# Two further expert-weight buffers laid over dead tiles in a one-core decoder layer with a routed feed-forward

## The chip, the cores and the metric

The kernel runs on one core of a Trainium2 chip. The core has a matrix engine (PE, with PEld for its weight loads), a vector engine (DVE), a scalar engine (ACT), GpSimd (POOL) and a queue engine (SP) that here only issues DMAs. The metric is the device time of one execution in microseconds (us); smaller is better. Engines run on their own and wait for each other through semaphores; each works through its own list of instructions in a fixed order.

## What is computed

A pre-norm decoder layer on 1024 tokens of width 512, all in float32. Cut to its three steps:

```python
x = x + attn(layernorm(x))                 # self-mixing over the batch axis
x = x + cross_attn(layernorm(x), ctx)      # 32 query heads, 8 key heads
x = x + ffn(layernorm(x))

def ffn(x):                                # x: 1024 x 512
    scores = sigmoid(x @ gate_w.T) + bias  # 16 experts
    w, idx = top_k(scores, 4); w = w / (w.sum() + 1e-20)
    out = sum over the 4 chosen experts e of  w_e * (silu(x @ Wg[e].T) * (x @ Wu[e].T)) @ Wd[e].T
    return out + silu(x @ Sg.T) * (x @ Su.T) @ Sd.T      # the shared expert
```

The change is about the routed experts. Each expert has three matrices of 512 KB (`Wg`, `Wu`, `Wd`), 1.5 MB together.

## The kernel before, in words

The program is written in a tile language: the author writes the operations in a source order, and a scheduler decides at build time in which order each engine's instructions stand and which semaphores they wait for. The order of the built program therefore need not be the order of the source, and a change in one engine's work can move instructions on another.

**Up to about 769 us** the two attention steps and the routing run. `xnT` (L101) is a 128 x 4 x 1024 tile that holds the normed tokens turned round; its last reader is the shared expert's first product (L885). `acc` (L102) is a 128 x 8 x 512 tile that holds the token sums; its last readers are the DMAs that write the layer's base result to the output (L904). Both tiles belong to the pool `keep` and stay allocated to the end.

**Routing** gives each expert the list of its tokens, cut into blocks of 128. There are at least 32 (`SURE`) and at most 47 (`NB`) blocks. On the first partition the kernel computes, per block, the expert's number and a flag `fresh` (L942 to L952): 1 where the weights must be loaded, 0 where the buffer already holds that expert. Both go into `steer`, which SP reads before each load.

**The main blocks** are the 32 sure ones (loop L1057 to L1070). They are taken in four lanes: step `j` works on block `8 * (j % 4) + j // 4`, with weight buffer `j % 4`. Neighbouring blocks of a lane mostly belong to one expert, so most loads have `fresh` 0 and are skipped. Step `j` has these parts on PE:

- X(j+1): four transposes of the gathered token rows `xg` into PSUM (L1005); ACT copies them to `xt` (L1007).
- Z(j-1): two transposes of the hidden rows `z` (L1025); DVE copies them to `zt` (L1027).
- H(j): the product of `xt` with `w1` (`Wg` and `Wu`), L1014; ACT takes the silu (L1018), DVE multiplies (L1019), which gives `z`.
- C(j-1): the product of `zt` with `w2` (`Wd`), L1034; ACT scales it to `y` (L1038).

POOL then touches `y` (L1041) and scatters it with an accumulating indirect DMA into the output (L1042); each scatter waits until the one before has landed. POOL also gathers the rows of later blocks (L996). X and Z share two PSUM banks (`tr`), which they take in turn, so the next X cannot start before ACT has copied the last X out of its bank.

**Loads.** `load_expert(j)` reads the expert's number and flag on SP and issues three conditional DMAs (L986) into `w1` and `w2` of the buffer; SP waits there until PE has finished with what the buffer held. At step `j` the load for step `j + 3` is issued. There are four buffers (`WB`, L970 and L971).

**The further blocks** (32 to 46) may or may not exist; they are done two at a time inside nested conditionals (`further`, L1083). They use the same four buffers, `(j - 1) % 4`. The load of block 33 stands at step 30 of the main loop, those of blocks 32, 34 and 35 behind the loop (L1067 to L1072), and inside `further` the loads of the two blocks after the next two stand behind the work of the pair (L1093). Block 32 shares its buffer with the last main block, so its flag compares its expert with that block's.

```python
def block(j):
    return SURE // WB * (j % WB) + j // WB if j < SURE else j
def buffer(j):
    return j % WB if j < SURE else (j - 1) % WB
```

Of the kernel before, what the change touches and what calls it, by code (L numbers as in the profile page):

```python
# [26 lines left out]
ALU = mybir.AluOpType  # L27
AX = mybir.AxisListType

P = 128  # L30
N, C, L = 16, 64, 512
NT = N * C // P
DC = L // P
KVH, GRP, HD = 8, 4, 128
E, FI = 16, 256
# [6 lines left out]
NB = 47  # L42
SURE = 32
WB = 4
ROUND = float(3 << 22)
HIGHEST = 3.0e38

# [2 lines left out]
def decoder_layer(  # L50
# [25 lines left out]
    V, S, T, G = nc.vector, nc.scalar, nc.tensor, nc.gpsimd  # L76
# [24 lines left out]
    xnT = keep.tile([P, DC, NT * P], F32, tag="xnT", name="xnT")  # L101
    acc = keep.tile([P, NT, L], F32, tag="acc", name="acc")  # L102
# [333 lines left out]
    for u in range(NT // 2):  # L436
        s = work.tile([P, 3, 2, P], F32, tag=f"xns{u}", name="xns", bufs=1)
# [310 lines left out]
    def routed_pair(u):  # L748
# [64 lines left out]
        V.tensor_scalar(col, got, 1.0 / P, (P - 1) / (2.0 * P), ALU.mult, ALU.subtract)  # L813
        V.tensor_scalar(col, col, ROUND, ROUND, ALU.add, ALU.subtract)
        row = route.tile([P, 2 * TOPK], F32, tag="row", name="row", bufs=1)
# [90 lines left out]
    def shared_half(th, queue):  # L906
# [33 lines left out]
    expert = route.tile([1, NB + 1], F32, tag="expert", name="expert")  # L940
    V.tensor_copy(expert, bp[:1, 128 : 128 + NB + 1])
    fresh = route.tile([1, NB + 1], F32, tag="fresh", name="fresh")  # L942
    V.memset(fresh, 1.0)
    runs, turns = (t[:, :SURE].rearrange("o (w r) -> o w r", w=WB) for t in (expert, fresh))
    V.tensor_tensor(turns[:, :, 1:], runs[:, :, 1:], runs[:, :, : SURE // WB - 1], ALU.not_equal)
    V.tensor_tensor(
        fresh[:, SURE : SURE + 1], expert[:, SURE : SURE + 1], expert[:, SURE - 1 : SURE], ALU.not_equal
    )
    V.tensor_tensor(
        fresh[:, SURE + WB :], expert[:, SURE + WB :], expert[:, SURE : NB + 1 - WB], ALU.not_equal  # L950
    )
    V.tensor_mul(fresh, fresh, bp[:1, 192 : 192 + NB + 1])  # L952
    in_use = route.tile([1, 1], F32, tag="inuse", name="in_use")
# [15 lines left out]
    moe = ctx.enter_context(tc.tile_pool(name="moe", bufs=2))  # L969
    w1_tiles = [moe.tile([P, 2, DC, FI], F32, tag=f"w1{b}", name="w1", bufs=1) for b in range(WB)]  # L970
    w2_tiles = [moe.tile([P, FI // P, L], F32, tag=f"w2{b}", name="w2", bufs=1) for b in range(WB)]  # L971

    def block(j):
        return SURE // WB * (j % WB) + j // WB if j < SURE else j

    def buffer(j):
        return j % WB if j < SURE else (j - 1) % WB

    def load_expert(j):
        b = block(j)  # L980
        e = nc.sync.value_load(steer[0:1, 0, b : b + 1], min_val=0, max_val=E - 1)
        new = nc.sync.value_load(steer[0:1, 1, b : b + 1], min_val=0, max_val=1)
        for dst, src in (
            (w1_tiles[buffer(j)][:, 0], wg), (w1_tiles[buffer(j)][:, 1], wu), (w2_tiles[buffer(j)], wd),
        ):
            nc.sync.dma_start(  # L986
                dst, src[bass.ds(e, 1)].rearrange("o p c f -> p (o c) f"), cond=(new != 0)
            )
# [4 lines left out]
    def gathered(j):  # L993
        b = block(j)
        xg = moe.tile([P, L], F32, tag="xg", name="xg", bufs=6) if j < SURE else xg_further[j % 4]
        G.indirect_dma_start(  # L996
            xg, None, rows_d, bass.IndirectOffsetOnAxis(idx[:, b : b + 1], axis=0)
        )
        return xg

    def rows_turned(j):
        xg = xgs.pop(j)
        tp = tr_bank()
        for d in range(DC):
            T.transpose(tp[:, d * P : (d + 1) * P], xg[:, d * P : (d + 1) * P], ident)  # L1005
        xt = moe.tile([P, DC, P], F32, tag="xt", name="xt", bufs=3) if j < SURE else xt_further[j % 4]
        S.copy(xt.rearrange("p d t -> p (d t)"), tp)  # L1007
        xts[j] = xt

    def hidden(j):  # L1010
        xt = xts.pop(j)
        hp = sc_bank()
        for d in range(DC):
            T.matmul(  # L1014
                hp, xt[:, d, :], w1_tiles[buffer(j)][:, :, d, :], start=(d == 0), stop=(d == DC - 1)
            )
        z = moe.tile([P, FI], F32, tag="z", name="z", bufs=3)
        S.activation(z, hp[:, :FI], AF.Silu)  # L1018
        V.tensor_mul(z, hp[:, FI:], z)  # L1019
        return z  # L1020

    def hidden_turned(z):
        tp = tr_bank()
        for c in range(FI // P):
            T.transpose(tp[:, c * P : (c + 1) * P], z[:, c * P : (c + 1) * P], ident)  # L1025
        zt = moe.tile([P, FI // P, P], F32, tag="zt", name="zt", bufs=3)
        V.tensor_copy(zt.rearrange("p c t -> p (c t)"), tp[:, :FI])  # L1027
        return zt

    def combined(j, zt):  # L1030
        b = block(j)
        op = mm_bank()
        for c in range(FI // P):
            T.matmul(  # L1034
                op, zt[:, c, :], w2_tiles[buffer(j)][:, c, :], start=(c == 0), stop=(c == FI // P - 1)
            )
        y = moe.tile([P, L], F32, tag="y", name="y", bufs=6)
        S.activation(y, op, AF.Copy, scale=weight[:, b : b + 1])  # L1038

        mark = xg_further[j % 4][:, :1] if SURE - 8 <= j < SURE - 4 else seen  # L1040
        G.tensor_copy(mark, y[:, :1])  # L1041
        G.indirect_dma_start(  # L1042
            out, bass.IndirectOffsetOnAxis(idx[:, b : b + 1], axis=0), y, None,
            bounds_check=NT * P - 1, oob_is_err=False, compute_op=ALU.add,
        )
# [11 lines left out]
    for j in range(SURE + 1):  # L1057
        if j + AHEAD < LAST:
            xgs[j + AHEAD] = gathered(j + AHEAD)
        rows_turned(j + 1)  # L1060
        zt = hidden_turned(zs.pop(j - 1)) if j > 0 else None
        if j < SURE:
            zs[j] = hidden(j)
        if zt is not None:
            combined(j - 1, zt)

        if j + WB - 1 < SURE:  # L1067
            load_expert(j + WB - 1)
        elif j == SURE - WB + 2:
            load_expert(SURE + 1)  # L1070
    for j in (SURE, SURE + 2, SURE + 3):
        load_expert(j)  # L1072

    blocks_used = nc.values_load(
        count[0:1, 0:1],
# [7 lines left out]
    def further(j0):  # L1083
        pair, later, last = ([j for j in (j0 + k, j0 + k + 1) if j < NB] for k in (0, 2, 4))
        with tc.If(blocks_used > j0):  # L1085
            for j in last:
                xgs[j] = gathered(j)
            for j in pair:
                z = hidden(j)
                if j + 2 < NB:  # L1090
                    rows_turned(j + 2)
                combined(j, hidden_turned(z))
            for j in last:  # L1093
                load_expert(j)
            if later:
                further(j0 + 2)

    further(SURE)


# [50 lines left out]
```

## Time and profile before

| what | value |
|---|---|
| time, median of 6 runs | 1000.67 us (998.75 to 1001.95) |
| the profiled execution's own time | 999.99 us |
| its span, first to last instruction | 998.2 us |
| mean granted PE clock | 0.995 |
| PE busy | 948.7 us (95% of the span) |
| DVE, ACT, POOL busy | 550.0, 441.7, 334.4 us |
| main blocks, PE (first H to the end of the loop) | 770.3 to 960.2 us |
| further blocks, PE | 960.2 to 985.1 us |
| scatters, gathers, load triples | 36, 40, 40 |

With 36 scatters, 36 blocks are in use: the 32 sure ones and four further ones (32 to 35). Of the 40 load triples most are skipped: on SP a DMA that is carried out takes about 0.34 us to issue, a skipped one about 0.08 us.

How to read it: a row of the timeline gives the start, the duration, the engine, the line, the operation, output <- input, and in brackets how long the engine had been idle before and what ended that. In a table of windows each engine has its busy time and number of instructions in that stretch, then come the PE clock (1.00 is full), the DMA engines' busy share and the rate. In a table of groups the idle time before a group's instructions stands last, with what ended it. Matmuls are pipelined, so the start of the next one, not the end of the last, tells how long one took.

### The profile page before, as it was taken

The numbers are of one execution on the slowest core, as the hardware profiler recorded it, in microseconds if no ns is written. First come the engines' busy times: TensorE is split into PE (matmuls) and PEld (weight loads), VectorE is DVE, ScalarE is ACT, GpSimd is POOL, SyncE is SP. The second block draws the span as 40 slices with busy tenths as digits, with TensorE's granted clock in tenths as the row PEclk, the third lists the DMA queues.
The fourth block names the chain that finished last, engine by engine and source line by source line (L and its number), as shares of the span: only waits on it lengthen the run. The fifth ranks groups of instructions, "written<-read, shape, count | busy, mean of one in ns | idle before, by whom it ended". The sixth has DMA issues, their size and how long they took to land. (4 is left out here: it accounts for less than half of the span.)

```text
span 998.2 us, 14858 instructions
## 1 busy us (share of the span) xinstructions
PE 948.7 (95%) x5080; PEld 659.1 (66%) x5080; DVE 550.0 (55%) x1194; ACT 441.7 (44%) x1258; POOL 334.4 (34%) x356
## 2 busy tenths in 40 slices
PE   8999998999999999999999989988999899999994
PEld 3456555888888888888888877776754445445442
DVE  4565657876767676758667667678574111111110
ACT  2366672654444454544544565655530222222221
POOL 2131102341613426135243242033053444444433
PEclk9999999999999999999999999999999999999997
DMA  9120015200201102012020110000034966655763
GB/s 238 70 96 22 11 33 104 107 2 1 85 1 43 43 1 86 1 54 85 1 85 1 44 43 1 22 23 22 22 105 159 349 147 150 156 108 119 195 178 67
DMA packets 28960, 76.88 MB, mean 77 GB/s; under 512 B 4624, under 2 KB 9024, under 8 KB 26832
## 3 DMA queue, kind: packets, MB, share of 16 engines
q1 hardware_dynamic: 18160, 52.96, 15.8%
q0 software_dynamic: 10432, 22.66, 10.7%
q8 instruction: 42, 0.69, 0.3%
q10 hardware_dynamic: 288, 0.26, 0.1%
q14 instruction: 38, 0.31, 0.1%
HBM read 102.31 MB, written 14.97 MB: 117 GB/s over the span
## 5 line engine op out<-in xcount | busy, mean ns | idle before, releaser
L1014 PE MATMUL sc<-w,xt 128*128 128x512 f32 x288 | 130.2, 593 | 2.8 <-DMA w<-in_wu_dram 2.8
L467 ACT ACTIVATE square<-qraw 128x128 f32<-128x128 f32 x256 | 79.0, 308 | 65.8 <-DVE qraw L463 38.7
L1014 PEld LDWEIGHTS sc<-w,xt 128*128 128x128 f32 x288 | 51.9, 190 | 54.3 <-issue 54.3
L229 POOL TENSOR_TENSOR sat<-at 128x256 f32<-128x256 f32 x24 | 17.5, 728 | 202.6 <-ACT at L580 202.6
L1019 DVE TENSOR_TENSOR z<-sc,z 128x256 f32<-128x256 f32 x36 | 15.3, 425 | 124.4 <-ACT z L1018 118.5
L255 PE MATMUL mm<-wq_sb,xnT 128*128 128x256 f32 x256 | 72.5, 389 | 0.0
L255 PE MATMUL mm<-wo_sb,at 128*128 128x256 f32 x256 | 66.0, 382 | 5.9 <-ACT at L580 5.9
L1034 PE MATMUL mm<-w,zt 128*128 128x512 f32 x144 | 68.0, 594 | 1.6 <-DVE zt L1027 1.6
L255 PE MATMUL mm<-wq_t,xns 128*128 128x256 f32 x256 | 66.3, 381 | 2.6 <-POOL wq_t L237 1.5
L1042 POOL DMA_INDIRECT out_dram<-y,idx x36 | 57.3, 1592 | 33.7 <-DMA out_dram<-y,idx 27.6
L255 PE MATMUL mm<-wo_t,sat 128*128 128x256 f32 x256 | 67.5, 383 | 0.0
L996 POOL DMA_INDIRECT xg<-rows_d,idx x40 | 39.6, 990 | 78.7 <-PE tr L1025 55.3
L840 POOL DMA_INDIRECT table_d<-entry_sb,at_slot x24 | 26.4, 1102 | 106.3 <-DVE at_slot L807 99.9
L1018 ACT ACTIVATE z<-sc 128x256 f32<-128x256 f32 x36 | 13.8, 383 | 107.2 <-PE sc L1014 104.5
L255 PEld LDWEIGHTS mm<-wo_sb,at 128*128 128x128 f32 x256 | 48.0, 190 | 13.9 <-ACT at L580 7.7
L255 PEld LDWEIGHTS mm<-wq_t,xns 128*128 128x128 f32 x256 | 48.4, 190 | 9.7 <-POOL wq_t L237 1.9
L255 PEld LDWEIGHTS mm<-wo_t,sat 128*128 128x128 f32 x256 | 47.6, 190 | 7.0 <-DVE sat L230 0.8
L1034 PEld LDWEIGHTS mm<-w,zt 128*128 128x128 f32 x144 | 27.1, 190 | 35.3 <-issue 32.0
L580 ACT COPY at<-sc 128x512 f32<-128x512 f32 x64 | 34.3, 588 | 31.6 <-PE sc L574 31.4
L493 DVE TENSOR_TENSOR qraw<-qraw,rs 128x512 f32<-128x512 f32 x64 | 47.9, 754 | 0.4
L255 PEld LDWEIGHTS mm<-wq_sb,xnT 128*128 128x128 f32 x256 | 44.4, 190 | 5.6 <-DVE su L459 0.3
L467 ACT ACTIVATION_READ_ACCUMULATOR square<-qraw 128x1 f32 x256 | 47.7, 186 | 0.0
(289 smaller groups left out, 2070.0 us busy)
## 6 DMA issues: line engine op xcount, KB each, us to landing
w<-in_wg_dram SPq DMA_DIRECT2D x40, 512.0 KB
w<-in_wu_dram SPq DMA_DIRECT2D x40, 512.0 KB
w<-in_wd_dram SPq DMA_DIRECT2D x40, 512.0 KB
wq_sb<-in_wq_dram SPq DMA_DIRECT2D x8, 1024.0 KB
wo_sb<-in_wo_dram SPq DMA_DIRECT2D x8, 1024.0 KB
xs<-in_x_dram SPq DMA_DIRECT2D x8, 256.0 KB
wv_sb<-in_wv_dram SPq DMA_DIRECT2D x2, 1024.0 KB
ct<-in_ctxt_dram SPq DMA_DIRECT2D x8, 256.0 KB
```

The costliest lines, as they stand in the source:

```text
L229: engine.tensor_add(s[:, 0], a21, a22)
L255: T.matmul(dst, left[:, k, :], right[:, k, :], start=k == 0, stop=k == 1)
L467: S.activation(square, raw[:, h, :], AF.Square, accum_out=q_ss[g][:, 2 * u + j, h : h + 1])
L493: V.tensor_mul(raw, raw, q_rs[g, i // 2][:, i % 2, :].unsqueeze(2).to_broadcast([P, GRP, HD]))
L580: S.copy(at[:, :, b * C : (b + 1) * C], pv[b].rearrange("p (a q) -> p a q", a=2 * GRP))
L840: G.indirect_dma_start(tables_d[q], bass.IndirectOffsetOnAxis(at_slots[u][:, q : q + 1], axis=0), entry_sb[:, 2 * u + j, k, :], None,)
L996: G.indirect_dma_start(xg, None, rows_d, bass.IndirectOffsetOnAxis(idx[:, b : b + 1], axis=0))
L1014: T.matmul(hp, xt[:, d, :], w1_tiles[buffer(j)][:, :, d, :], start=(d == 0), stop=(d == DC - 1))
L1018: S.activation(z, hp[:, :FI], AF.Silu)
L1019: V.tensor_mul(z, hp[:, FI:], z)
L1034: T.matmul(op, zt[:, c, :], w2_tiles[buffer(j)][:, c, :], start=(c == 0), stop=(c == FI // P - 1))
L1042: G.indirect_dma_start(out, bass.IndirectOffsetOnAxis(idx[:, b : b + 1], axis=0), y, None, bounds_check=NT * P - 1, oob_is_err=False, comp ...
```

## The change

Two more weight buffers are added. They take no new memory: each is cut out of a tile that is no longer needed (`xnT` and `acc`; 12 KB of the 16 KB that each has per partition). The further blocks use all six buffers (`WF`), `(j - 32 + 4) % 6`: block 32 the one over `xnT`, block 33 the one over `acc`, 34 to 37 the four old ones. So the flags change: blocks 32 to 37 are always loaded if they exist, and later ones are compared with the block six before; one small DVE instruction falls away. The loads move in the source: block 32's to step 16 and block 33's to step 18 of the main loop, 34's and 35's to steps 29 and 30, and those inside `further` ahead of the pair's work.

```diff
 SURE = 32
 WB = 4
+WF = 6
...
     V.tensor_tensor(turns[:, :, 1:], runs[:, :, 1:], runs[:, :, : SURE // WB - 1], ALU.not_equal)
     V.tensor_tensor(
-        fresh[:, SURE : SURE + 1], expert[:, SURE : SURE + 1], expert[:, SURE - 1 : SURE], ALU.not_equal
-    )
-    V.tensor_tensor(
-        fresh[:, SURE + WB :], expert[:, SURE + WB :], expert[:, SURE : NB + 1 - WB], ALU.not_equal
+        fresh[:, SURE + WF :], expert[:, SURE + WF :], expert[:, SURE : NB + 1 - WF], ALU.not_equal
     )
...
+    for spare in (xnT, acc):
+        flat = spare.rearrange("p a b -> p (a b)")
+        w1_tiles.append(flat[:, : 2 * DC * FI].rearrange("p (s d f) -> p s d f", s=2, d=DC))
+        w2_tiles.append(flat[:, 2 * DC * FI : 2 * DC * FI + FI // P * L].rearrange("p (c l) -> p c l", l=L))
...
     def buffer(j):
-        return j % WB if j < SURE else (j - 1) % WB
+        return j % WB if j < SURE else (j - SURE + WB) % WF
...
         if j + WB - 1 < SURE:
             load_expert(j + WB - 1)
-        elif j == SURE - WB + 2:
-            load_expert(SURE + 1)
-    for j in (SURE, SURE + 2, SURE + 3):
-        load_expert(j)
+        elif j < SURE - 1:
+            load_expert(j + WB + 1)
+        if j in (SURE // 2, SURE // 2 + 2):
+            load_expert(SURE + (j - SURE // 2) // 2)
...
             for j in last:
                 xgs[j] = gathered(j)
+                load_expert(j)
             for j in pair:
                 z = hidden(j)
                 if j + 2 < NB:
                     rows_turned(j + 2)
                 combined(j, hidden_turned(z))
-            for j in last:
-                load_expert(j)
             if later:
                 further(j0 + 2)
```

Three lines are added ahead of L1014 in sum, so L1014 of the kernel before is L1017 of the changed one, and so on for the lines of the block loop.

## The prediction

> **What bounds the kernel now.** I read the table of windows first, to see which engine is full in the stage that the change touches. Columns after the window: its length, then PE, PEld, DVE, ACT and POOL busy, the PE clock, the DMA share, GB/s.
>
> ```profile
> 769.00:790.00 21.00, 17.88 (x61) 9.03 (x60) 3.24 (x7) 5.23 (x10) 7.57 (x10) 1.00 1.03 401
> 790.00:957.80 167.80, 167.80 (x521) 83.37 (x519) 24.21 (x57) 44.18 (x86) 77.15 (x84) 1.00 0.60 146
> 957.80:985.20 27.40, 25.78 (x77) 12.19 (x76) 3.82 (x9) 7.03 (x14) 12.83 (x14) 1.00 0.64 184
> ```
>
> From 790 to 957.8 us PE is busy 167.80 of 167.80 us: it never waits for a weight load, and whatever delays PE there delays the end. The groups of PE in the third window say what its 1.6 us of idle time are:
>
> ```profile
> L1014 PE MATMUL sc<-w,xt 128*128 128x512 f32 x32 | 14.7, 593 | 0.0
> L1034 PE MATMUL mm<-w,zt 128*128 128x512 f32 x20 | 9.7, 608 | 1.6 <-DVE zt L1027 1.6
> ```
>
> Product H, the first reader of a load, waits 0.0 us; the 1.6 us are three waits of C for DVE's copy, no load. SP's timeline shows when the further loads go out (0.08 us is a skipped DMA, 0.34 us one carried out):
>
> ```profile
> 955.50 0.08 SPq L986 DMA_DIRECT2D w<-in_wg_dram  x1
> ...
> 960.79 0.34 SPq L986 DMA_DIRECT2D w<-in_wg_dram  x1
> ...
> 964.19 0.33 SPq L986 DMA_DIRECT2D w<-in_wd_dram  x1
> ```
>
> Block 32's load is skipped (its expert is block 31's). 34's and 35's go out from 960.79 to 964.52, late, behind 32's. But H(34) starts at 972.57 and H(35) at 976.44 with no wait. **The waits that the change is made against do not exist with this data.**
>
> **The change part by part.**
>
> *Earlier loads: 0.* Nothing waits for them today. Their cover is the 8 us between 964.5 and 972.57; nothing is late next.
>
> *One extra load (block 32, 1.5 MB), and 33 earlier: 0.* SP issues them behind step 16's and step 18's own loads (their last DMAs stand at 870.10 and 881.71), six more issues of 0.34 us, 2 us of SP, which idles between loads. Behind them on SP stand the loads of steps 20 and 22, which have two steps to land and are skipped. The DMA share was 0.44 to 0.67 in 867 to 890 us. Beside a load a scatter takes longer: the one at 796.85 was followed at 804.16 (7.3 us), one without a load at 809.11 by the next at 814.07 (5.0 us). So each load puts POOL 2.3 us behind, and POOL makes up 0.8 us per 5.81-us step. Scatters reach PE only through six `y` buffers; the gathers, also on POOL, are issued some 30 us ahead of use (911.43 the last main one, used at about 945). A lag of even 5 us is hidden; uncovered, a load would cost 2.3.
>
> *New waits on SP.* The load into `acc` waits for DMAs issued by POOL at 768 to 772 and landed 100 us earlier: 0.
>
> *The DVE instruction removed:* starts 0.07 us apart (758.76, 758.83) ahead of the first load, which PE later waits for (2.14 and 0.65 us at 776 and 783). Worth -0.1 if issue time binds, 0 if bandwidth does (401 GB/s then). I take -0.1.
>
> *The built order of PE: this is the cost.* The new loads make the scheduler place the transposes of steps 22 to 25 differently, though the source does not ask for it. Comparing the two built programs, PE's order is the same up to Z(21), then
>
> before: X(23) Z(21) **H(22) C(21)** X(24) Z(22) H(23) C(22) X(25) Z(23) H(24) C(23) ...
> after: X(23) Z(21) **first of X(24), C(21), H(22), rest of X(24), Z(22)**, X(25) H(23) C(22) Z(23) half of X(26) H(24) C(23) rest of X(26) Z(24) H(25) ...
>
> and the same again from X(27). Two places lose their cover. The rows of the regular order give the latencies:
>
> ```profile
> 898.94 0.60 PE L1005 MATMUL tr<-ident,xg 128*128 128x128 f32 x4
> 899.38 0.38 PE L1025 MATMUL tr<-ident,z 128*128 128x128 f32 x2
> 899.60 1.88 PE L1014 MATMUL sc<-w,xt 128*128 128x512 f32 x4
> 899.78 0.58 ACT L1007 COPY xt<-tr 128x512 f32<-128x512 f32 x1
> 899.80 0.42 DVE L1027 COPY zt<-tr 128x256 f32<-128x256 f32 x1 [1.53 <-PE tr L1025]
> ```
>
> (a) X(24) needs the bank from which ACT is still copying X(23). The copy ends at 899.78 + 0.58 = 900.36; PE would be free at 899.60. From DVE's copy ending at 958.29 to PE's start at 958.35 it is 0.06 us, so PE restarts at 900.42: 0.82 us lost, and about 0.08 for an emptied pipeline (first product after a wait 0.07 to 0.10 longer, as 3.50 for 3.43 us at 783.38). `zt` (900.22) is ready by then. Sum 0.90.
>
> (b) Z(22) now follows H(22) with only three transposes between instead of C (1.72 us) and X. How long `z` takes:
>
> ```profile
> 951.87 3.60 PE L1014 MATMUL sc<-w,xt 128*128 128x512 f32 x8
> 955.50 0.38 ACT L1018 ACTIVATE z<-sc 128x256 f32<-128x256 f32 x1 [2.88 <-PE sc L1014]
> 955.92 0.42 DVE L1019 TENSOR_TENSOR z<-sc,z 128x256 f32<-128x256 f32 x1 [3.43 <-ACT z L1018]
> ```
>
> `z` is done 4.47 us after H starts, PE can use it at 4.53. H itself takes 3.43 (to 955.30), three transposes 0.32, so PE waits 4.53 - 3.75 = 0.78, plus 0.08: 0.86.
>
> Behind these the cover is back: X(25) waits for ACT's copy of X(24), ready about 0.2 us before it is due; Z(23) and Z(24) follow H and C, 5.15 us after H's start, 0.62 more than needed. So 0.
>
> POOL's list changes too (one scatter ahead of a gather, steps 26 and 27); both have the lead named above: 0. The order inside the conditionals is the same.
>
> *The tail.* The last scatter starts when the one before has landed:
>
> ```profile
> 977.53 1.60 POOL L1042 DMA_INDIRECT out_dram<-y,idx  x1 [3.08 <-DMA out_dram<-y,idx]
> ...
> 983.66 1.62 POOL L1042 DMA_INDIRECT out_dram<-y,idx  x1 [0.60 <-issue]
> ...
> 989.03 1.59 POOL L1042 DMA_INDIRECT out_dram<-y,idx  x1 [2.81 <-DMA out_dram<-y,idx]
> ```
>
> The scatter at 977.53 is late because 34's and 35's loads ran beside the earlier ones; with earlier loads it gains up to 3.08. But the next, at 983.66, waited for no DMA: it follows PE's C(34). So 0; the tail moves with PE.
>
> **Sum:** 0.90 + 0.86 - 0.1 = +1.66 on the profiled execution's 999.99 (span 998.2 plus 1.8 around it): 1001.65. The median of the runs shown is 0.68 higher, so 1000.67 + 1.66 = **1002.3 us**. About 0.2%, 2.0 us, is what a measurement of this kernel can tell from no change; the forecast lies just inside. Ends of the unknown: 0 if the reordered places cost nothing, 0.9 + 0.86 + two more of 0.85 if the next two Z are uncovered too.
>
> The Trainium skill, *Perfetto Trace Analysis*, section *Optimization Strategy*, says that the same gap repeating on the engine that should be full can mean too few buffers. Its condition meets the three equal gaps of 0.52 us in the third window; by the rule the two buffers would take away 1.6 us and the time would be about 1000.7. The row names DVE's copy, not a buffer, as what ended them, so I leave them in.
>
> **Rivals.**
> 1. *Slower by more.* At the moved places of steps 23 and 24 the silu-multiply chain is not covered either: from where it exceeds 5.15 us after H's start (4.53 now; ACT's list there also has two copies in a row) each adds up to 0.85. Sum +1.7 + 1.7 - 0.1: 1004.0. For it: PE has no slack to give back. Against: 0.62 us of margin.
> 2. *Nothing lost.* Transposes are moved into time that is idle anyway, or only one of the two waits shows: +0 to +0.8, about 1001.0. For it: an earlier X(24) can run while PE would wait. Against: PE waits nowhere there.
> 3. *Faster.* The scatter chain does set the end, and the loads' early landing gives back the 3.08 us of its wait: -3.1 + 0.9, about 998.4. It decides if the row at 983.66 was bound by landing. Against: its idle time is put to issue.
>
> **How the numbers follow.** Forecast 0.62 (of it 0.22 above 1002.67, as the runs scatter by 1 to 2 us around a value that lies 0.35 below), rival 1 0.16, rival 2 0.16, rival 3 0.06. Slower by over 0.2%: 0.22 + 0.16 = 0.38; within: 0.40 + 0.16 = 0.56; faster 0.06. The range leaves out rival 3 and the outer halves of the others' scatter: 1000.2 to 1004.2.
>
> **What would show it.** In the profile after: PE idle in steps 21 to 23, some 895 to 910 us, of about 0.8 before an L1008 transpose (released by ACT) and 0.8 before an L1028 transpose (by DVE), and nowhere else new; H never waiting for a load; C(34)'s scatter 1.7 us later than 983.66. I am wrong if PE stays at 100% there, if H waits for a DMA after 870, or if the tail shortens.

## The result and the profile after

| | before | changed |
|---|---|---|
| median | 1001.75 us (52 runs, 998.75 to 1005.52) | 1003.1 us (24 runs, 1002.14 to 1006.2) |
| ratio to before, 95% interval | 1 | 1.0017 [1.001, 1.0025] |
| profiled span | 998.2 us | 1000.3 us |
| start of H(2) | 783.38 us | 783.73 us |
| from H(2) to the start of the last C | 199.77 us | 201.48 us |
| from there to the start of the last scatter | 5.88 us | 5.67 us |

The changed kernel is slower by about 1.7 us by the ratio (its interval allows 1.0 to 2.5; the medians alone differ by 1.35). Ratios are of fast runs: the one slow run here, 1909.98 us in e10 below, is left out of its ratio. The stretches in the table start and end with these rows, first of the kernel before, then of the changed one:

```profile
783.38 3.67 PE L1014 MATMUL sc<-w,xt 128*128 128x512 f32 x8 [0.65 <-DMA w<-in_wu_dram]
...
983.15 1.98 PE L1034 MATMUL mm<-w,zt 128*128 128x512 f32 x4 [0.52 <-DVE zt L1027]
```

```profile
783.73 3.67 PE L1017 MATMUL sc<-w,xt 128*128 128x512 f32 x8 [0.89 <-DMA w<-in_wu_dram]
...
985.21 1.98 PE L1037 MATMUL mm<-w,zt 128*128 128x512 f32 x4 [0.52 <-DVE zt L1030]
```

The windows of the changed kernel (length, then PE, PEld, DVE, ACT, POOL busy, PE clock, DMA share, GB/s), split around the place that the prediction named, show where the time goes:

```profile
790.00:895.00 105.00, 105.00 (x326) 52.24 (x325) 15.54 (x37) 28.13 (x55) 49.40 (x54) 1.00 0.67 176
895.00:912.00 17.00, 15.75 (x49) 7.71 (x48) 1.75 (x5) 4.17 (x8) 6.75 (x9) 1.00 0.63 161
912.00:957.80 45.80, 45.80 (x141) 22.51 (x140) 6.75 (x16) 11.75 (x23) 20.08 (x23) 1.00 0.68 179
957.80:985.20 27.40, 25.86 (x82) 12.61 (x80) 4.25 (x10) 7.62 (x15) 12.62 (x14) 1.00 0.36 73
```

PE, busy throughout the main blocks from 790 us on before, is now idle in one of these windows, 895 to 912 us, where before it was busy 17.00 of 17.00. PE's timeline there (start, duration, line, operation; in brackets the idle time and what ended it):

```profile
899.74 0.38 PE L1028 MATMUL tr<-ident,z 128*128 128x128 f32 x2
900.76 0.33 PE L1008 MATMUL tr<-ident,xg 128*128 128x128 f32 x1 [0.65 <-ACT xt L1010]
900.93 1.89 PE L1037 MATMUL mm<-w,zt 128*128 128x512 f32 x4
902.66 3.60 PE L1017 MATMUL sc<-w,xt 128*128 128x512 f32 x8
906.09 0.49 PE L1008 MATMUL tr<-ident,xg 128*128 128x128 f32 x3
907.19 0.44 PE L1028 MATMUL tr<-ident,z 128*128 128x128 f32 x2 [0.61 <-DVE z L1022]
```

The reader sees the two named places: the first transpose of X(24) waits for ACT's copy of X(23), and Z(22), with only three transposes between it and H(22), waits for `z`. Read by starts, since the ends are modelled: Z(21) at 899.74 takes 0.22, so X(24) was due at 899.96 and starts 0.80 later, and is itself 0.06 longer; Z(22) was due at 906.09 + 0.32 = 906.41, starts 0.78 later, and takes 0.05 longer. That is 0.86 + 0.83 = 1.69 us; from H(2) to the last C the trace grew by 1.71. The starts themselves are those of the prediction's latencies: X(23) starts at 899.30, and 1.48 behind it (898.94 to 900.42 in the prediction) is 900.78, for 900.76; H(22) at 902.66 + 4.53 is 907.19.

The further blocks wait for the same thing as before (groups in 957.8 to 985.2 us; idle time and its releaser last):

```profile
L1017 PE MATMUL sc<-w,xt 128*128 128x512 f32 x16 | 7.4, 593 | 0.0
L1037 PE MATMUL mm<-w,zt 128*128 128x512 f32 x12 | 5.7, 601 | 0.5 <-DVE zt L1030 0.5
L1017 PE MATMUL sc<-acc,xt 128*128 128x512 f32 x8 | 3.8, 593 | 0.0
L1037 PE MATMUL mm<-acc,zt 128*128 128x512 f32 x4 | 2.0, 619 | 0.5 <-DVE zt L1030 0.5
```

The third of these waits, 0.52 us, belongs to the C at 985.21, just behind the window. H reads the new buffers (here the one over `acc`) with no wait, as it read the old ones. The loads that were to help are on SP at the main blocks, carried out (0.34 us each):

```profile
872.43 0.34 SPq L989 DMA_DIRECT2D xnT<-in_wg_dram  x1
...
883.67 0.34 SPq L989 DMA_DIRECT2D acc<-in_wg_dram  x1
```

And the tail on POOL stands as far behind the last C as it did:

```profile
978.34 1.59 POOL L1045 DMA_INDIRECT out_dram<-y,idx  x1 [2.37 <-DMA out_dram<-y,idx]
...
985.72 1.62 POOL L1045 DMA_INDIRECT out_dram<-y,idx  x1 [0.60 <-issue]
...
990.88 1.58 POOL L1045 DMA_INDIRECT out_dram<-y,idx  x1 [2.60 <-DMA out_dram<-y,idx]
```

The scatter at 985.72 follows C(34) by issue alone, 2.06 us later than before's 983.66 (1.71 of it behind H(2)).

### The profile page after: what moved, and what is told of

Read it like the earlier page. It is cut to its first block, busy times and chain, and to the rows that moved or that the text cites. A ratio compares the mean times of both kernels' runs of the same rounds, so it can differ in the third digit from the quotient of the medians.

```text
span 1000.3 us, 14854 instructions
## 1 busy us (share of the span) xinstructions
PE 950.0 (95%) x5080; PEld 659.4 (66%) x5080; DVE 551.6 (55%) x1193; ACT 441.6 (44%) x1258; POOL 334.3 (33%) x356
## 5 line engine op out<-in xcount | busy, mean ns | idle before, releaser
L1017 PE MATMUL sc<-w,xt 128*128 128x512 f32 x272 | 122.9, 594 | 2.1 <-DMA w<-in_wu_dram 1.9
L1017 PEld LDWEIGHTS sc<-w,xt 128*128 128x128 f32 x272 | 49.1, 190 | 51.5 <-issue 49.9
L1037 PE MATMUL mm<-w,zt 128*128 128x512 f32 x136 | 64.1, 594 | 1.0 <-DVE zt L1030 1.0
L1041 ACT ACTIVATE y<-mm,weight 128x512 f32<-128x512 f32 x36 | 24.7, 687 | 52.2 <-PE mm L1037 40.5
L523 PEld LDWEIGHTS sc<-kT,qt 128*64 128x64 f32 x1024 | 33.5, 137 | 21.7 <-DVE qt L511 17.1
```

What stands on the lines that cost most here:

```text
L523: T.matmul(sp[h * C : (h + 1) * C, at : at + C], qt[:, b, 2 * hp + h, :], kT[g // 4][:, g % 4, k0 : k0 + C], start=True, stop=True,)
L1017: T.matmul(hp, xt[:, d, :], w1_tiles[buffer(j)][:, :, d, :], start=(d == 0), stop=(d == DC - 1))
L1037: T.matmul(op, zt[:, c, :], w2_tiles[buffer(j)][:, c, :], start=(c == 0), stop=(c == FI // P - 1))
```

## The experiments

**Theory.** PE's built order costs the 1.7 us; the loads, the buffers and their waits cost nothing. **Rivals.** The loads beside the main blocks cost something of their own; the buffers do; what happens ahead of H(2) does.

All runs in one table. "C" is the start of the last C, "S" the start of the last scatter, both counted from the start of H(2) in the one profiled execution, in us. The ratio is to runs of the kernel before on the same chip. "Reserve" is by how much the rows of block 36 could still come later before X(36) waits: from the issue of their gather to X(36), less the 4.07 that this took where X(36) did wait (e5: 975.82 to 979.89; it was 4.16 in e7 and 4.65 in e12, so a reserve is good to some 0.6). Below zero it is the wait itself. Block 36 is not in use with this data: X(36) turns rows that no H reads, and PE waits for them only because X(36) stands ahead of its next products.

| kernel | H(2) starts | C | S | reserve | ratio [95%] |
|---|---|---|---|---|---|
| before | 783.38 | 199.77 | 205.65 | 6.6 | 1 |
| changed | 783.73 | 201.48 | 207.15 | 5.2 | 1.0017 [1.001, 1.0025] |
| e1 spread | 785.17 | 199.78 | 205.45 | 2.9 | 1.0022 [1.0006, 1.0038] |
| e2 skip two | 786.31 | 201.48 | 206.92 | 5.6 | 1.0012 [0.9995, 1.0028] |
| e3 buffers alone | 784.35 | 199.77 | 205.90 | 1.4 | 1.0009 [0.9994, 1.0024] |
| e4 z first | 784.22 | 198.46 | 204.65 | 5.3 | 0.9993 [0.9976, 1.001] |
| e5 spread, z first | 786.03 | 200.60 | 208.05 | -1.9 | 0.9992 [0.998, 1.0004] |
| e6 loads at 8 and 10 | 786.81 | 202.45 | 208.03 | 2.9 | 1.0023 [1.0011, 1.0035] |
| e7 eight loads | 786.63 | 207.25 | 213.12 | -5.4 | 1.0072 [1.0053, 1.0091] |
| e8 before again | 787.68 | 199.78 | 205.60 | 6.5 | one run |
| e9 eight loads, early gathers | 784.66 | 199.78 | 214.04 | - | 1.0091 [1.0074, 1.0109] |
| e10 e5, early gathers | 786.54 | 198.47 | 205.85 | - | 1.0006 [0.9995, 1.0017] |
| e11 e4, early gathers | 786.43 | 198.47 | 204.63 | - | 1.0002 [0.9989, 1.0016] |
| e12 spread again | 782.39 | 201.26 | 207.57 | -1.3 | 1.0011 [0.9995, 1.0027] |

### Same loads, PE's order put back: e1 and e12

```diff
-        if j in (SURE // 2, SURE // 2 + 2):
-            load_expert(SURE + (j - SURE // 2) // 2)
+        if j in (16, 24):
+            load_expert(SURE + (j == 24))
```

With block 33's load at step 24 in place of 18, the built order of PE is that of before.

> The changed kernel with block 33's load at step 24 in place of step 18; all else as changed. In the built program PE's order is then that of the kernel before, while the extra 1.5 MB and all earlier loads stay. Theory A (the transposes moved in steps 22 to 25 cost the time): the two waits of 0.65 and 0.61 us near 900 us are gone, PE is busy without a gap from 790 us to the end of the main blocks, and the time is that of before within 0.1%, ratio 0.9990 to 1.0010. Theory B (the extra and earlier loads cost it, through DMA traffic): ratio near 1.0017 as for the changed kernel, with PE idle before a product H.

In the trace both waits are gone, PE is busy throughout 790 to 958 us, and C stands at 199.78, before's value to 0.01 us. PE's timeline of this kernel at the same steps:

```profile
901.17 0.38 PE L1028 MATMUL tr<-ident,z 128*128 128x128 f32 x2
901.39 3.60 PE L1017 MATMUL sc<-w,xt 128*128 128x512 f32 x8
904.83 1.88 PE L1037 MATMUL mm<-w,zt 128*128 128x512 f32 x4
```

Z, H, C follow without idle time. But the ratio, 1.0022, did not fall: the theory's time (0.9990 to 1.0010) was missed. So it was timed again:

> The kernel of e1_spread (block 33's load at step 24, PE's order that of before), timed a second time. Theory (from H(2) on it is before's equal, and the ratio 1.0022 of the first time was what single executions differ by ahead of H(2)): from H(2) to the last C 199.77 again, the last scatter starting 205.3 to 206 us behind H(2); ratio 1.000, give or take 0.0015. Rival A (something ahead of H(2) is later in every execution of the kernels with the freed rows, such as addresses or the missing DVE instruction): ratio 1.002 again. Rival B (the early load puts the scatter chain behind the last C in most executions, and the first profile missed it): last scatter 207 us or more behind H(2), ratio 1.002.

The second profiled execution shows what the first did not: X(36), the transposes of a further block's rows, waits for its gather.

```profile
976.48 0.63 PE L1008 MATMUL tr<-ident,xg 128*128 128x128 f32 x4 [1.29 <-DMA xg<-rows_d,idx]
```

POOL issued that gather at 971.83, 189.44 us behind H(2); in e1 it was 185.67, in before 181.93. The same kernel, then, loses nothing here in one execution and 1.5 us (C 201.26) in another. This gives rival B of e12 a mechanism, which is argued and not shown alone: the loads among the main blocks put POOL's chain of scatters behind, and at step 24 there is less time left to make it up than at 18. There is a second source. The change also moves 34's and 35's loads beside the last main scatters; there two scatters of e12 stand 9.14 us apart (946.14 and 955.28). In e6 below the chain has made up its two loads by 935.81 (149.00 us behind H(2); before has 146.33, and PE lost 2.68), and still its gather of block 36 goes out 188.35 us behind H(2), 3.7 later than before's 181.93 and the 2.68 account for (in e2, where only 34's and 35's loads are left, 1.0 later than PE accounts for). How much of e12's lateness is of which source no run shows. Nor does it follow that the late chain is all of the two ratios: 1.0022 and 1.0011 stand for some 1.6 us, the two traces (S -0.2 and +1.9) for 0.9 on average, and both intervals are some 3 us wide.

### Same order, two loads skipped: e2

```diff
+    V.memset(fresh[:, SURE : SURE + 2], 0.0)
     V.tensor_mul(fresh, fresh, bp[:1, 192 : 192 + NB + 1])
```

> The changed kernel with its PE order, but the flags of blocks 32 and 33 set to 0, so that their two loads (3 MB) are skipped; the two blocks then compute with whatever lies in the old tiles, so this part of the output is left out of the comparison. Theory A: order alone costs, so ratio 1.0017 (1.0007 to 1.0027) and both waits near 900 us remain, 0.6 to 0.9 us each. Theory B: without the traffic the time falls back to before, ratio 1.000, and the waits are gone.

C stands at 201.48 exactly as in the changed kernel, with the same waits (0.65 and 0.61 us): in the trace the two loads add nothing to the path of PE, and leaving them out gives nothing back:

```profile
903.34 0.33 PE L1009 MATMUL tr<-ident,xg 128*128 128x128 f32 x1 [0.65 <-ACT xt L1011]
...
909.76 0.44 PE L1029 MATMUL tr<-ident,z 128*128 128x128 f32 x2 [0.61 <-DVE z L1023]
```

The ratio, 1.0012 [0.9995, 1.0028], agrees with that and cannot tell it apart from no change.

### The buffers alone: e3

The two buffers and the flags of the change, the loads at the places that they have before.

```diff
-        elif j < SURE - 1:
-            load_expert(j + WB + 1)
-        if j in (SURE // 2, SURE // 2 + 2):
-            load_expert(SURE + (j - SURE // 2) // 2)
+        elif j == SURE - WB + 2:
+            load_expert(SURE + 1)
+    for j in (SURE, SURE + 2, SURE + 3):
+        load_expert(j)
...
                 xgs[j] = gathered(j)
-                load_expert(j)
...
+            for j in last:
+                load_expert(j)
```

> Only the two buffers and the flags are changed; every load stands where it stood in the kernel before. PE's built order is that of before. Block 32 is now loaded (1.5 MB more) behind the main loop, just ahead of the loads of 34 and 35. Theory A: block 32's load goes out early, because its buffer is free and SP reaches it at about 950 us; ratio 0.999 to 1.001. Theory B: about as slow as the changed kernel. A third outcome: if SP gets to block 32's load only at about 946 to 950 us, it must land before H(32) at 960; if it does not, PE waits there for some us (up to 5).

C 199.77, no wait near 900 us: behind H(2) the buffers cost PE nothing. The ratio, 1.0009 [0.9994, 1.0024], can be told neither from 1 nor from 1.0017, and the missing DVE instruction acts ahead of H(2), where this trace can't show it. What the buffers do cost is reserve, 1.4 us for 6.6: block 32's load is now carried out (from 945.01 us), 34's goes out 13 us earlier than in the kernel before (163.98 us behind H(2) for 177.41), and two of the last main scatters stand 8.48 us apart (950.70 and 959.18).

### Another place, another order: e6

The same edit as in e1 with steps 8 and 10. The scheduler then builds an order that the prediction's rules can be tried on afresh.

> The changed kernel with the loads of blocks 32 and 33 at steps 8 and 10 in place of 16 and 18. Built order: X(15) Z(13), first of X(16), C(13), rest of X(16), H(14), Z(14), X(17), half of C(14), H(15), half of C(14), Z(15), X(18), H(16), C(15), Z(16). Theory (order of PE decides): X(16) waits for ACT's copy of X(15), 0.85 in all as at X(24) in the changed kernel; Z(14) directly behind H(14) waits 4.53 - 3.43 = 1.10 for z, 1.18 with the refill; C(14) behind X(17) 0.1; Z(15) behind H(15) and half of C, 4.29 us, 0.24 and 0.3 with the refill. Sum 2.4: from H(2) to the last C 199.77 + 2.4 = 202.2 us, and no wait in 895 to 912 us. Rival A (loads beside main blocks cost, wherever the order stands): 201.5 as in the changed kernel. Rival B (a moved transpose costs PE only in that one place, steps 21 to 23, where something else runs): 199.8. Time: theory 1.0024, A 1.0017, B 1.000, each give or take 0.002.

```profile
857.39 0.33 PE L1008 MATMUL tr<-ident,xg 128*128 128x128 f32 x1 [0.65 <-ACT xt L1010]
...
864.14 0.44 PE L1028 MATMUL tr<-ident,z 128*128 128x128 f32 x2 [0.93 <-DVE z L1022]
```

C is 202.45: +2.68 for +2.4 expected (most of the 0.28 at C(14) behind X(17), which started 0.24 late and took 0.10 longer, for 0.1 expected). The waits stand 46.5 us earlier, counted from H(2) (857.39 - 786.81 for 900.76 - 783.73), which is the eight steps of 5.81 us by which the order changes earlier, and the rivals' values (201.5, 199.8) are missed. This is the strongest support for the theory: a cost computed from the built order and three latencies, for an order not yet run.

### The cost of a load beside the main blocks: e7 and e9

```diff
     V.tensor_tensor(turns[:, :, 1:], runs[:, :, 1:], runs[:, :, : SURE // WB - 1], ALU.not_equal)
+    V.memset(turns[:, :, 4:6], 1.0)
```

The kernel before, with seven loads more in steps 13 to 20 (of the eight forced ones, one was made anyway).

> The kernel before, but the weights of all eight blocks of steps 16 to 23 are loaded, though some of them lie in the buffers already (their flags are set to 1); PE's order as before, the output the reference's. Theory (loads beside the main blocks cost PE nothing, since they land two steps ahead and scatters are not waited for): 199.8 from H(2) to the last C, PE busy throughout 790 to 957 us, scatters of that stretch up to 4 us or more behind their issue; time 1.000 give or take 0.002. Rival A (a load costs PE by itself, half of the changed kernel's 1.7 us for each added one): 199.8 plus 0.85 for each added load, 203 for four of them. Rival B (the scatters' lag fills the six buffers of y, and C's bank comes free late): waits of C for ACT's y at 870 to 900 us.

The theory was right up to 957 us (PE busy in 790 to 957.8, no wait for `y`) and wrong behind it: ratio 1.0072, C 207.25. PE, and below it POOL, in that kernel:

```profile
984.81 1.09 PE L1006 MATMUL tr<-ident,xg 128*128 128x128 f32 x4 [5.38 <-DMA xg<-rows_d,idx]
985.69 4.22 PE L1015 MATMUL sc<-w,xt 128*128 128x512 f32 x6
```

```profile
978.78 1.56 POOL L1043 DMA_INDIRECT out_dram<-y,idx  x1 [3.34 <-DMA out_dram<-y,idx]
980.65 1.03 POOL L997 DMA_INDIRECT xg<-rows_d,idx  x1 [0.30 <-issue]
```

The gather of block 36 stands on POOL behind the last main scatters, each of which waits until the one before has landed. It is issued 194.02 us behind H(2), in place of 181.93: 12.1 us for seven loads, 1.7 each. X(36) starts 5.5 us late, and the stretch behind the pause is 1.9 us longer (9.07 us from X(36) to the last C for 7.14 before), because the clock fell.

To see whether this gather was the cause, the rows of 36 and 37 were given buffers of their own and gathered amid the last main steps (cut to its main lines):

```diff
+    rest = acc.rearrange("p a b -> p (a b)")[:, 6 * L :]
+    xg_further += [rest[:, k * L : (k + 1) * L] for k in range(2)]
...
         if j + AHEAD < LAST:
             xgs[j + AHEAD] = gathered(j + AHEAD)
+        if j in (SURE - 2, SURE - 1):
+            xgs[j + 6] = gathered(j + 6)
```

> The kernel with all eight blocks of steps 16 to 23 loaded, and two more row buffers (in the free token accumulator), so that the rows of blocks 36 and 37 are gathered behind 35's amid the last main steps, ahead of the last main scatters in POOL's list, not behind them. PE's order and the loads as with the eight loads. Theory (the loads cost PE nothing where they stand; they put POOL's scatters late, and the gather of block 36, queued behind the last main scatter, came 5.38 us late for X(36), with a slower clock behind the wait): no wait of X(36), from H(2) to the last C 199.8 again in place of 207.25; time 1.000 to 1.002 of before instead of 1.0072, the rest being the last scatter, which may still come late. Rival (the 7.5 us come from the late scatters or the loads themselves, not through this gather): still 204 or more, with a wait elsewhere (C for a buffer of y, or H for a load), ratio 1.005 to 1.007.

The theory's first half holds to 0.01 us: C 199.78, no wait for rows. Its second half falls: the ratio stays, 1.0091. POOL's last two scatters:

```profile
993.46 1.62 POOL L1045 DMA_INDIRECT out_dram<-y,idx  x1 [0.72 <-DMA out_dram<-y,idx]
...
998.70 1.59 POOL L1045 DMA_INDIRECT out_dram<-y,idx  x1 [3.42 <-DMA out_dram<-y,idx]
```

PE started its last C at 984.44; the last scatter starts 14.26 us behind it, where before has 5.88. Here the chain of scatters sets the end, each one waiting for the one before to land. The late gather was a symptom of that chain, and curing it moved the wait to the tail.

### The three waits of 0.52 us: e4, e5, e10, e11

In the last main step and in the second block of each further pair, Z goes ahead of X (e4: on the kernel before).

```diff
-        rows_turned(j + 1)
+        if j < SURE:
+            rows_turned(j + 1)
         zt = hidden_turned(zs.pop(j - 1)) if j > 0 else None
+        if j == SURE:
+            rows_turned(j + 1)
...
-                if j + 2 < NB:
-                    rows_turned(j + 2)
-                combined(j, hidden_turned(z))
+                if j == pair[0]:
+                    if j + 2 < NB:
+                        rows_turned(j + 2)
+                    combined(j, hidden_turned(z))
+                else:
+                    zt = hidden_turned(z)
+                    if j + 2 < NB:
+                        rows_turned(j + 2)
+                    combined(j, zt)
```

> The kernel before, with one thing changed: in the last main step and in the second block of each further pair the two transposes of z stand ahead of the four transposes of the gathered rows, not behind them. These are the three places where PE waits 0.52 us for DVE's copy of z. The four transposes (0.43 us) then run while DVE copies. Theory A in its general form (what counts is what stands between a product and the transposes that need its result): each wait falls by 0.43 us, sum -1.3 us, ratio 0.9987. Rival: z is not ready at the earlier place, so that the wait only changes its place: ratio 1.000.

The profile shows none of the three waits any more, C is 198.46, 1.31 us less. PE's last rows, for the waits that the prediction showed:

```profile
981.78 0.38 PE L1025 MATMUL tr<-ident,z 128*128 128x128 f32 x2
982.00 0.60 PE L1005 MATMUL tr<-ident,xg 128*128 128x128 f32 x4
982.68 1.98 PE L1034 MATMUL mm<-w,zt 128*128 128x512 f32 x4
```

X now covers most of DVE's copy. Read by starts, C was due at 982.00 + 0.44 = 982.44 and starts 0.24 later; before it was due at 982.25 + 0.22 = 982.47 and started 0.68 later. So 0.44 of each wait is covered, as expected. No buffer was needed for it. S gained 1.00 of the 1.31, since the last scatter waits a little longer for the one before. The ratio, 0.9993 [0.9976, 1.001], is of the right size and cannot be told from no change.

> The changed kernel with two edits together: block 33's load at step 24 (PE's order of the main steps is again that of before), and in the last main step and the second block of each further pair the transposes of z go ahead of those of the gathered rows. Theory (the order of PE decides, loads cost PE nothing): from the start of H(2) to the start of the last C 198.46 us, as with the order alone and 1.3 less than before (199.77); no wait in 790 to 957 us and no wait of 0.52 behind it; time 0.999 of before, give or take 0.002 for what happens ahead of H(2). Rival A (the loads among the main blocks cost something of their own, and the ratio 1.0022 of the spread loads was theirs): 198.46 plus 1 to 2 us, ratio 1.001 to 1.002. Rival B (the three waits move to another place when the further loads come early): 199.8.

The three waits went, but X(36) waited 1.94 us for its gather, so C was 200.60. None of the three readings named that. The profiled execution was the slowest of its eleven (1005.1 us; their median 1001.0), so how often X(36) waits there is not known; the ratio, 0.9992, is the theory's.

> The changed kernel with block 33's load at step 24, z's transposes ahead of the rows' in the last main step and in each further pair's second block, and the early gathers of blocks 36 and 37. Theory (three causes, each with its own cure: the order of PE, the three waits for DVE's copy, the late gather): no wait of PE between 790 us and the last C at all, 198.46 from H(2) to the last C in place of 200.60; time 0.998 to 1.000 of before, by what precedes H(2). Rival (the late gather was scatter of one execution and the move of it shows nothing): 198.46 too, but then X(36) would have had its rows in time with the gather behind the last main scatter as well; if the wait stays with the gather issued early, the cause is the transfer and not the queue.

No wait of PE behind H(2)'s, C 198.47, as the theory had it. But S is 205.85 for before's 205.65: with the early loads the chain of scatters takes the whole gain of PE back (in e11, without them, S is 204.63). The ratio, 1.0006, is not below 1 as forecast.

> The kernel before (four weight buffers, no early load) with z's transposes ahead of the rows' in the last main step and in the second block of each further pair, and the early gathers of blocks 36 and 37. A candidate that keeps what the runs showed to be worth something and leaves out the two weight buffers. Theory: 198.46 from H(2) to the last C as with the order alone (X(36) had its rows in time there), ratio 0.9985 to 0.9995, no better than the order alone. Rival (the early gathers put the scatters of the last steps late, two gathers of 1 us and their traffic being ahead of them now): last C as said, but the last scatter 1 us or more later behind it, ratio 1.000.

C 198.47 and S 204.63 as in e4, ratio 1.0002, above the forecast 0.9985 to 0.9995: no better, and with e4 beside it no version here is shown to beat the kernel before. What e4 does to 0.1% is below what was measured.

### What a single execution differs by: e8

> The kernel before, unchanged, one more profiled execution. Theory (what happens ahead of H(2) differs between single executions of the same kernel): from H(2) to the last C again 199.77 within 0.05, while H(2) starts anywhere between 783.4 and 786.5 us, not at 783.38 again within 0.1. Rival (the start of H(2) is a property of the kernel, and the changed kernels with 783.7 to 786.3 lose up to 2.9 us ahead of it): H(2) at 783.4 within 0.2.

H(2) starts at 787.68 in place of 783.38, beyond the theory's range; C is 199.78 again. So the stretch ahead of H(2) differs by 4.3 us between two executions of one kernel, while the 200 us behind it repeat to 0.01. The span alone could not have shown a cost of 1.7 us; the stretch from H(2) could. That the new buffers delay H(2) is not to be seen either: it starts at 785.17 us on average in the eight executions with them and at 785.50 in the six without, though a shift of 1 us could hide in this scatter.

## Why the prediction was right, and where not

The sum was +1.66 us; the ratio, 1.0017 of 1001.75, is +1.7. That the two agree to a tenth is luck in part, as the ratio's interval runs from 1.0 to 2.5 us and the tenth taken off for the DVE instruction is not shown by any run. That the median is 1003.1 and not 1002.3 lies in the base: six runs of before had 1000.67, all 52 have 1001.75.

- **The built order (0.90 + 0.86): right, and shown in the traces.** Measured by starts 0.86 and 0.83, together 1.69 of the 1.71 that PE lost. e1 (order put back, same loads: 199.78), e2 (order kept, loads skipped: 201.48) and e6 (another order: +2.68 for 2.4) separate it from the loads. The times alone don't: with the order put back the ratio stayed at 1.0022 and 1.0011, and with the loads skipped it was 1.0012. Z(23) and Z(24) were covered, so rival 1 did not happen; X(24) could not run in idle time, so rival 2 did not either.
- **"Earlier loads: 0": right.** H waited for no load in the further blocks, before or after. That they also delay the last main scatters (e3, e6) the step did not see; in the changed kernel's trace this cost nothing.
- **"One extra load ... 0": right for this kernel's trace, too broad as an argument.** e2 shows that the two loads cost PE nothing there. But the step rested on gathers "issued some 30 us ahead of use". One gather is not: that of block 36, behind the last main scatters, is issued 10.7 us ahead of X(36) (965.31 to 976.01). Its reserve was 6.6 us and fell to 5.2. "A lag of even 5 us is hidden" came out near the true limit by luck, since it was not worked out from this gather; e5, e7 and e12 are past it. Whether some executions of the changed kernel pass it too is open: one was profiled.
- **"Each load puts POOL 2.3 us behind": the right order, not the right size.** Beside block 32's load two scatters stand 9.25 us apart (872.62 and 881.87), 4.2 more than the 5.0 without a load; over seven loads (e7) what remained at the end was 1.7 each.
- **The DVE instruction (-0.1): not to be seen.** H(2) starts anywhere between 782.39 and 787.68 us in fourteen executions, so that a tenth cannot be read there. The changed kernel's +0.35 at H(2) says nothing either.
- **The tail (0): right.** 5.67 us behind the last C for 5.88. Rival 3's chain does set the end where the loads are many (e9) or PE is faster (e10), and it shows in e12 and e5 too, where the last scatter stands 6.31 and 7.45 us behind the last C; then it costs, and does not give back.
- **The rule on repeated gaps.** The Trainium skill, *Perfetto Trace Analysis*, section *Optimization Strategy*, says that such a gap can mean a want of buffers. The three gaps of 0.52 us are no such case as far as weight buffers go: with six in place of four they stayed, 0.52 each; with two steps put in another order (e4) they went. The row's releaser, DVE's copy, decided it.

## What to carry to other kernels

Where a scheduler orders the engines, compare the built order of the full engine before costing a change to anything else: here two loads that nobody waited for moved a few transposes, and the price followed from where each lost its cover (copy out of the bank, or product to transposed input). A transfer is free only while every chain that it slows has a reserve left; find the shortest lead behind that chain (here one gather and the last scatter), not the usual one. And when the effect is 2 us and the start differs by 4, measure between two instructions inside the kernel.

## What the runs showed of the hardware

- **A pause of 5.38 us costs PE more than the pause.** Behind it, in e7, the granted clock was half:

```profile
984.80:988.40 3.60, 3.59 (x8) 2.05 (x9) 0.00 (x0) 0.59 (x1) 0.87 (x3) 0.50 0.35 50
```

  Six products of H took 4.06 us (985.69 to 989.75) in place of 2.58 (976.44 to 979.02 before). Behind pauses of 1.29 and 1.94 us (e12, e5) the four transposes took 0.63, hardly more than 0.60. The Trainium skill, *TensorE: Matmul & The Clock Gate*, section *Part 1: The HAM clock gate*, says that the array runs at half rate after an idle window of about 3.4 us, until one such window has been busy. The way back agrees roughly: the clock is full again from 988.7 us, 3.9 behind PE's restart at 984.81. The fall came sooner than 3.4 us: the clock is 1.00 up to 981.5 and 0.50 from 982.0, which is 2.1 to 2.6 us behind the end of the last product (979.43, a modelled end).
- **Here loads slowed the accumulating scatters and not PE's products:** seven loads more (e7) left PE at 100% in 790 to 957.8 us and put POOL 12.1 us late.
- **How late the scatters are differs between executions of one kernel:** 185.67 and 189.44 us from H(2) to the same gather (e1, e12), though PE, up to H(34), keeps time to 0.01 (189.20 us behind H(2) in both).
